# A delta-rule sandwich kernel: sums of a variance and its epsilon from GpSimd to ScalarE, and a list of their own for the steps of blocks between the chain's steps

## The chip, the cores and the metric

The kernel runs on one NeuronCore of a Trainium2 chip. The metric is the device time of one execution in microseconds (us). Of the kernel before, three runs are given: 2363.38, 2366.94 and 2370.86 us, median 2366.94. One further execution was taken with the hardware profiler; times inside the kernel come from it.

The engines are named as in the profile: PE is TensorE's matmuls and PEld its weight loads, DVE is VectorE, ACT is ScalarE, POOL is GpSimd, and SP is SyncE, on whose queue nearly all DMAs are issued. Each engine works through its instructions in the order in which they were issued to it.

## The reference

The input x is 4 sequences of 4096 tokens with 512 features, in float32. Two sublayers are computed, each as x + layernorm(f(layernorm(x))).

```python
# first sublayer, on h = layernorm(x): 16 heads of 32 features
rk = h_heads / max(norm(h_heads), 1e-12)      # keys to read with
wk = rk of the token before (zero for the first)
v = h @ Wv.T;  gate = sigmoid(h @ Wg.T);  beta = sigmoid(h @ Wb.T)
for each token t:                             # S: 32x32 state per sequence and head
    err = (v_t - wk_t @ S) * beta_t
    S   = S + outer(wk_t, err)
    o_t = (rk_t @ S) * gate_t
f(h) = o @ Wo.T
# second sublayer, on h = layernorm(x1)
xn = layernorm(h, eps 1e-3) * ln_gamma + ln_beta
w_q = weight rounded to -1, 0, 1;  y = clip(xn * 128 / gamma) @ w_q, scaled back
```

Every layernorm needs, for each token, a power -0.5 of a variance plus an epsilon: one number in each of 128 partitions.

## The kernel before, in words

**Units and the two halves of the work.** A unit is 32 tokens of each of the 4 sequences: 128 rows, one per partition. There are 128 units. Inside a unit the recurrence over 32 tokens is solved at once: a triangular 32x32 matrix per sequence and head (`nat`) is formed and inverted, and its inverse is applied to the unit. What belongs to a unit alone is the work of the *blocks*: load x, normalise (`x_stats`, `x_norm`, `keys`), transpose (`keys_turn`), norms of the keys (`key_squares`, `key_sums`, `key_norms`), values and gates (`values`, `values_out`, `values_rest`), the matrix (`grams`, `blocks`, `writes`, `masked`). What needs the state of the unit before is the *chain*: `predict` (ps_r, then r = v - ps_r), `apply` (ps_u), `errors` (ps_f, then e and o), `grow` (ps_ds, then the state), and behind it the output projection (`project`, `residual`), the second layernorm (`x1_stats`, `x1_norm`, `x1_turn`, `x1_scale`), the ternary matmul (`ternary_a`, `ternary_b`) and `finish`.

**The inverses.** The matrices of a group of units are inverted together on VectorE, by pairs of instructions (`pr` at L359, then `na` at L365) and a last copy of ones (L370). Groups have 4, 4, 6, 6 and then 8 units. The matrices pass through DRAM: `masked` stores them (`nat_d`), `gather` (L346) loads two units' worth into one of two buffers `na`, `keep` (L389) stores the inverted ones (`q_d`), and `fetch_inverse` (L396) loads them for the chain.

**What sets the order.** The order on every engine is written out by hand: `in_order` chains every instruction behind the one before on its engine. A *step* has a unit i of the chain, or none, and a unit k of the blocks. For each step a list of items is walked (L820 to L837): `plan` for a step of the chain, `late` once no blocks are left (k > 128), and `lead` for a step without a chain. An item names a function and which unit it is for; a bare number is a share of the inverse, and `inverses` issues as many of its instructions as make up that share of the group's due in this step. The first ten steps are without a chain. Then come units -2 and -1 of the chain, and from unit 0 to unit 7 every step of the chain is followed by one without it (a pair), until the blocks are 20 units ahead; from unit 8 on every step has both. For each group, `spans` holds the steps during which it is inverted, and `moves` says at the end of which step each gather and keep is issued.

**Sums of a variance and its epsilon.** They are made for each unit at four places: in `x_norm` (L171, `vpe_a`), in `project` through `rstd_of` (L100, `vpe_b`), in `x1_stats` (L556, `vpe_c`) and in `ternary_b` (L614, `vpe_y`). Each is a POOL instruction on 128x1 elements and is followed by POOL's power (L172, L95). `x_norm` also makes the negative mean, `negm`, on POOL (L173) and `nba` from it (L174). The variances of b, c and y come from ScalarE: `squares` (L522) squares 512 columns and reads an accumulator; those of a come from VectorE (L107). `rstd_b` is what VectorE's `residual` (L545, `xr`) waits for. Further down POOL's queue are the copy into `hN` (L202), which `values` needs, and `gates` (L305).

The buffers: PSUM has four rotating banks and one tile of four banks, which ps_gram and ps_ds share. The small tiles (`vpe`, `acc`, `mv`) rotate through six buffers each.

Of the kernel before, what the change touches and what calls it, by code (L numbers as in the profile page):

```python
# [8 lines left out]
F32 = mybir.dt.float32  # L9
AF = mybir.ActivationFunctionType  # L10
ALU = mybir.AluOpType
AX = mybir.AxisListType

P = 128
LN_EPS_OUTER = 1e-5
LN_EPS_FFN = 1e-3
# [6 lines left out]
def kernel(  # L23
# [22 lines left out]
    nc = tc.nc  # L46
    B, T, D = x.shape
# [3 lines left out]
    NU = T // DH  # L51
# [4 lines left out]
    const = ctx.enter_context(tc.tile_pool(name="const", bufs=1))  # L56
# [21 lines left out]
    negm = const.tile([P, NU], F32, name="negm")  # L78
# [4 lines left out]
    wq = const.tile([P, KC, D], F32, name="wq")  # L83
    beta = const.tile([P, 1], F32, name="beta")
    eps2 = const.tile([P, 1], F32, name="eps2")

    def bcast(ap, shape, axis):
        return ap.unsqueeze(axis).to_broadcast(shape)
# [4 lines left out]
    def power(pool, t, name):  # L93
        r = pool.tile([P, 1], F32, tag="rstd", name=f"rstd_{name}")
        nc.gpsimd.tensor_tensor(r, t, mhalf[:, 0:1], ALU.pow)  # L95
        return r

    def rstd_of(pool, var, eps, name):
        t = pool.tile([P, 1], F32, tag="vpe", name=f"vpe_{name}")
        nc.gpsimd.tensor_scalar_add(t, var, eps)  # L100
        return power(pool, t, name)

    def mean_var(pool, src, name):
# [6 lines left out]
    with ExitStack() as ph1:  # L110
# [24 lines left out]
        stat = ph1.enter_context(tc.tile_pool(name="stat", bufs=6))  # L135
        cx = [{} for _ in range(NU)]

        sizes = [4, 4, 6, 6]
        NP = 4
# [6 lines left out]
        half = D // 2  # L146
# [20 lines left out]
        def x_norm(i):  # L167
            mv = cx[i].pop("mv")
            c = slice(i, i + 1)
            t = stat.tile([P, 1], F32, tag="vpe", name=f"vpe_a{i}")  # L170
            nc.gpsimd.tensor_scalar_add(t, mv[:, 1:2], LN_EPS_OUTER)  # L171
            nc.gpsimd.tensor_tensor(rsa[:, c], t, mhalf[:, 0:1], ALU.pow)  # L172
            nc.gpsimd.tensor_scalar_mul(negm[:, c], mv[:, 0:1], -1.0)  # L173
            nc.gpsimd.tensor_tensor(nba[:, c], negm[:, c], rsa[:, c], ALU.mult)  # L174

        def normed(h, xt, i):
# [227 lines left out]
        def inverses(share):  # L404

            inv["due"] += share / inv["steps"]
            while inv["ops"] is not None and inv["done"] < inv["due"] - 1e-9:
                d = next(inv["ops"], None)
                if d is None:
                    inv["ops"] = None  # L410
                else:
                    inv["done"] += d
# [118 lines left out]
        def project(i):  # L531
            my = cx[i]
            oT = my.pop("oT")
            my["ps_wo"] = ps = bank(f"ps_wo_{i}")
            for k in range(KC):
                nc.tensor.matmul(  # L536
                    ps, lhsT=oT[:, k, :], rhs=woT[:, k, :], start=(k == 0), stop=(k == KC - 1)
                )
            var = squares(i, ps, "b", scale=D**-0.5)
            my["rs_b"] = rstd_of(stat, var, LN_EPS_OUTER, f"b{i}")  # L540

        def residual(i):
            my = cx[i]
# [6 lines left out]
        def x1_stats(i):  # L550

            my = cx[i]

            var = squares(i, my["x1"], "c", bias=negm[:, i : i + 1])
            t = stat.tile([P, 1], F32, tag="vpe", name=f"vpe_c{i}")
            nc.gpsimd.tensor_scalar(  # L556
                t, var, (1.0 + LN_EPS_FFN) / D, LN_EPS_OUTER * LN_EPS_FFN, ALU.mult, ALU.add
            )
            rs = power(stat, t, f"c{i}")
            nb = stat.tile([P, 1], F32, tag="nb", name=f"nb_c{i}")  # L560
            nc.gpsimd.tensor_tensor(nb, negm[:, i : i + 1], rs, ALU.mult)
            my["rs"], my["nb"] = rs, nb
# [44 lines left out]
        def ternary_b(i):  # L607
            my = cx[i]
            ternary_half(i, range(KC // 2, KC))
            my.pop("xn")  # L610
            ps = my["ps_y"]
            var = squares(i, ps, "y", scale=D**-0.5)
            t = stat.tile([P, 1], F32, tag="vpe", name=f"vpe_y{i}")
            nc.gpsimd.tensor_tensor(t, var, eps2, ALU.add)  # L614
            my["rs_y"] = power(stat, t, f"y{i}")

        def finish(i):
            my = cx[i]
# [76 lines left out]
        def ternary_centre():  # L695
# [13 lines left out]
        BACK, AHEAD = "chain's unit", "unit of the blocks"  # L709
        plan = (  # L710
            (AHEAD, 4, load), (BACK, 2, fetch), (BACK, 2, fetch_inverse), (BACK, 2, again),
            (BACK, 0, predict), (AHEAD, -1, blocks), (AHEAD, -1, writes), (BACK, -1, out_turn),
            (BACK, -3, x1_turn),
            (BACK, 0, apply), (BACK, -3, x1_scale), (AHEAD, -1, masked),
            (AHEAD, 1, key_sums), (AHEAD, 3, x_stats), (AHEAD, 1, key_norms),
            (AHEAD, 2, keys), (AHEAD, 2, key_squares), 0.38,
            (BACK, -4, ternary_a), (BACK, 0, errors), (BACK, -4, ternary_b), (BACK, 0, outputs),
            (AHEAD, 3, x_norm), 0.2, (BACK, 0, grow), (BACK, -2, x1_stats),
# [21 lines left out]
            (AHEAD, 2, keys_turn), (AHEAD, -1, gates_first), (AHEAD, -2, gates), (AHEAD, 0, grams), 0.3,  # L740
        )


        FAR = 4 * NP + 4
        START = sizes[0] + 6
        steps = [(None, k) for k in range(START)]

        k = START - 1
# [6 lines left out]
        at_k = {k: n for n, (_, k) in enumerate(steps)}  # L755
        at_i = {i: n for n, (i, _) in enumerate(steps) if i is not None}
        spans, moves = [], {}
        for g, (f, n) in enumerate(zip(firsts, sizes)):
            begin = max(at_k[f + n] + 2, spans[-1][1] if g else 0)
            end = at_i[f - 2]  # L760
            assert begin < end
            spans.append((begin, end))

            free = spans[g - 2][1] + sizes[g - 2] // 2 - 1 if g > 1 else 0
            for a in range(n // 2):
                free = max(at_k[f + 2 * a + 2], free)
                assert free < begin
                moves.setdefault(free, []).append((gather, g, a))
                moves.setdefault(end - 1 + a, []).append((keep, g, a))
                free += 1  # L770

        traced = nc.cur_bb.bb.instructions
# [47 lines left out]
        for n, (i, k) in enumerate(steps):  # L820
            for g, (begin, end) in enumerate(spans):
                if begin == n:
                    inv.update(ops=invert(g), done=0.0, due=0.0, steps=end - begin)
            for item in lead if i is None else plan if k <= NU else late:
                if isinstance(item, float):
                    inverses(item)
                    continue
                base = i if item[0] == BACK else k
                if base is not None:
                    do(item[2], base + item[1], *item[3:])  # L830
            if any(end == n + 1 for _, end in spans):
                inverses(1.0)
            for f, g, a in moves.get(n, ()):
                f(g, a)
            for f in between.get(n, ()):
                f()
            seen = in_order(seen)  # L837
# [31 lines left out]
        place, both, again_ = some(1), some(2), some(1)  # L869
# [121 lines left out]
```

## Time and profile before

| | before |
|---|---|
| median of three runs | 2366.94 us |
| the profiled execution | 2368.07 us |
| its span, first to last instruction | 2366.3 us |
| PE busy | 2239.2 us (95%), 22563 matmuls |
| DVE busy | 2034.9 us (86%) |
| ACT busy | 1734.6 us (73%) |
| POOL busy | 1726.8 us (73%) |
| granted TensorE clock, mean | 0.978 |

By stage (busy us of each engine):

| stretch, us | PE | DVE | ACT | POOL | granted clock |
|---|---|---|---|---|---|
| 0 to 60 | 43.50 | 36.93 | 42.53 | 42.50 | 0.94 |
| 60 to 120 | 34.74 | 52.80 | 28.51 | 50.40 | 0.83 |
| 120 to 180 | 49.66 | 46.72 | 36.36 | 46.39 | 0.80 |
| 180 to 240 | 48.13 | 50.22 | 34.99 | 47.16 | 0.80 |
| 240 to 300 | 54.69 | 50.43 | 41.83 | 50.23 | 0.94 |
| 300 to 360 | 53.96 | 51.18 | 41.27 | 50.06 | 0.94 |
| 600 to 1000 | 395.64 | 359.74 | 313.20 | 317.61 | 1.00 |
| 2300 to 2366 | 53.91 | 25.78 | 29.50 | 16.37 | 0.92 |

How to read the lines that follow in this document: a line of the order in time has its start and its length in us, the engine, the line of the program and the operation, output and inputs by the program's names, their shapes and the number of instructions; in square brackets is how long the engine stood idle before it and what released it. SPq is SP's queue, where DMAs are issued. The page's slices cut the span into 40 equal parts and give busy tenths, and the granted clock in tenths of full speed.

### The profile page before, as it was taken

To read this page: it belongs to the slowest core of one execution; us is meant where nothing else is said; L and a number is where in the kernel's file an instruction comes from. 1 tells how busy PE (TensorE), PEld (TensorE's weight loads), DVE (VectorE), ACT (ScalarE), POOL (GpSimd) and SP (SyncE) were. 2 spreads that over 40 slices of the span, in tenths; PEclk is the share of its full clock that TensorE was granted. 3 is DMA by queue.
4 is the path that set the end of the run, shared out by engine and by line. 5 is a ranking of instruction groups with operands and counts; after the bars stand their busy time and mean duration, and the time that the engine had idled before them with its cause. 6 is when DMAs were issued, how large, how long until landed. Compare 5 with 4: busy or idle time off the path is not lost.

```text
span 2366.3 us, 60183 instructions
## 1 busy us (share of the span) xinstructions
PE 2239.2 (95%) x22563; PEld 1459.4 (62%) x22563; DVE 2034.9 (86%) x3068; ACT 1734.6 (73%) x3485; POOL 1726.8 (73%) x2695
## 2 busy tenths in 40 slices
PE   7687889999999999999999999999999999989997
PEld 5465656656666666666666666666666666655553
DVE  6878888988898898989899898989989898899863
ACT  7466667777777777877777787877778787766774
POOL 7877887877878787877878787787878788643322
PEclk9878999999999999999999999999999999999999
DMA  6586577787878868787887878778787977776752
GB/s 186 136 187 171 161 187 188 192 187 188 187 212 192 221 178 209 203 188 213 191 219 179 212 197 197 207 192 215 180 214 197 198 203 191 193 170 160 188 154 85
DMA packets 753107, 445.27 MB, mean 188 GB/s; under 512 B 578832, under 2 KB 578832, under 8 KB 752816
## 3 DMA queue, kind: packets, MB, share of 16 engines
q1 hardware_dynamic: 752432, 440.90, 74.5%
q8 instruction: 178, 2.92, 0.5%
q14 instruction: 113, 0.93, 0.1%
q10 hardware_dynamic: 384, 0.52, 0.1%
HBM read 205.07 MB, written 235.14 MB: 186 GB/s over the span
## 4 chain that ended last, share of the span: by engine, by line
PE 73%; DVE 12%; POOL 5%; ACT 3%; issue 3%; DMA 2%; SPq 2%; ACTq 0%; DVEq 0%; POOLq 0%
PE ps_y L599 16%; PE ps_wo L536 15%; PE ps_v L246 8%; PE ps_v L274 7%; PE ps_ds L493 6%; PE ps_u L457 5%; PE ps_gram L314 4%; DVE pr L359 4%; PE ps_r L441 4%; PE ps_hT L191 3%; DVE na L365 3%; PE ps_oT L516 2%; PE ps_f L470 2%; PE ps_xn L516 1%; DVE r L447 1%
## 5 line engine op out<-in xcount | busy, mean ns | idle before, releaser
L599 PE MATMUL ps_y<-wq,xn 128*128 128x512 f32 x1024 | 502.9, 615 | 0.0
L359 DVE TENSOR_TENSOR pr<-na 128x336 f32<-128x336 f32 (+25 forms) x540 | 464.6, 860 | 18.3 <-DMA na<-nat_d 7.0
L325 ACT COPY nat<-ps_gram 32x512 f32<-32x512 f32 x512 | 295.2, 577 | 239.2 <-PE ps_gram L314 233.8
L536 PE MATMUL ps_wo<-woT,oT 128*128 128x512 f32 x1024 | 467.2, 599 | 0.4 <-ACT oT L529 0.4
L365 DVE TENSOR_TENSOR na<-na,pr 128x336 f32<-128x336 f32 (+25 forms) x540 | 454.3, 841 | 12.2
L226 POOL TENSOR_TENSOR rn<-ss,mhalf 128x16 f32<-128x16 f32 x128 | 425.7, 3326 | 10.7
L499 DVE TENSOR_TENSOR state<-ps_ds,state 32x512 f32<-32x512 f32 x508 | 348.4, 686 | 28.4 <-PE ps_ds L493 22.2
L430 ACT COPY tbd<-q 32x512 f32<-32x512 f32 x512 | 313.1, 611 | 7.0
L333 POOL TENSOR_TENSOR nat<-nat,mb 128x512 f32<-128x512 f32 x122 | 162.0, 1328 | 198.8 <-issue 190.0
L536 PEld LDWEIGHTS ps_wo<-woT,oT 128*128 128x128 f32 x1024 | 186.7, 192 | 190.0 <-issue 186.8
L246 PE MATMUL ps_v<-wvbT,hN 128*128 128x288 f32 x1024 | 280.8, 419 | 19.9 <-POOL hN L202 19.9
L599 PEld LDWEIGHTS ps_y<-wq,xn 128*128 128x128 f32 x1024 | 177.0, 193 | 152.6 <-issue 150.0
L246 PEld LDWEIGHTS ps_v<-wvbT,hN 128*128 128x128 f32 x1024 | 198.5, 196 | 116.9 <-issue 34.9
L274 PE MATMUL ps_v<-wvbT,hN 128*128 128x256 f32 x1024 | 242.9, 380 | 0.0
L274 PEld LDWEIGHTS ps_v<-wvbT,hN 128*128 128x128 f32 x1024 | 195.9, 191 | 34.2
L493 PEld LDWEIGHTS ps_ds<-e,h 32*128 32x128 f32 x4064 | 128.9, 191 | 111.2 <-DVE e L473 77.1
L581 ACT ACTIVATE xn<-ps_xn,lnb,lng 128x128 f32<-128x128 f32 x512 | 193.2, 465 | 0.2 <-PE ps_xn L516 0.2
L457 PE MATMUL ps_u<-tbd,r 128*32 128x128 f32 x4096 | 143.1, 282 | 47.9 <-DVE r L447 47.9
L545 DVE SCALAR_TENSOR_TENSOR xr<-ps_wo,rstd_b,xr 128x512 f32<-128x512 f32 x128 | 96.1, 750 | 98.9 <-POOL rstd_b L95 94.6
L493 PE MATMUL ps_ds<-e,h 32*128 32x128 f32 x4064 | 153.6, 289 | 15.0 <-DVE e L473 15.0
L522 ACT ACTIVATE junk_y<-ps_y 128x512 f32<-128x512 f32 x128 | 76.4, 597 | 120.0 <-PE ps_y L599 120.0
L457 PEld LDWEIGHTS ps_u<-tbd,r 128*32 128x32 f32 x4096 | 107.5, 112 | 71.1 <-DVE r L447 43.7
(152 smaller groups left out, 4027.2 us busy)
## 6 DMA issues: line engine op xcount, KB each, us to landing
x<-in_L_attn_x_dram SPq DMA_DIRECT2D x256, 128.0 KB
hT_d<-hT SPq DMA_DIRECT2D x128, 256.0 KB
v_d<-v SPq DMA_DIRECT2D x128, 256.0 KB
nat_d<-nat SPq DMA_DIRECT2D x128, 256.0 KB
na<-nat_d SPq DMA_DIRECT2D x256, 128.0 KB
q_d<-na SPq DMA_DIRECT2D x64, 512.0 KB
v<-v_d SPq DMA_DIRECT2D x128, 256.0 KB
hT<-hT_d SPq DMA_DIRECT2D x128, 256.0 KB
```

The costliest lines, as they stand in the source:

```text
L226: nc.gpsimd.tensor_tensor(rn, ss, mhalf, ALU.pow)
L246: nc.tensor.matmul(ps[:, : half + 2 * H], lhsT=my["hN"][:, k, :], rhs=wvbT[:, k, half:], start=(k == 0), stop=(k == KC - 1),)
L274: nc.tensor.matmul(ps[:, :half], lhsT=my["hN"][:, k, :], rhs=wvbT[:, k, :half], start=(k == 0), stop=(k == KC - 1),)
L325: nc.scalar.copy(nat[s].rearrange("p (j q) t -> p j q t", j=HQ), ps[s].rearrange("p j (q t) -> p j q t", q=NQ)[:, :, :, s],)
L359: nc.vector.tensor_tensor(prs[s], bcast(na[:, :, s, s + 1 :], [P, np_, s, m], 2), bcast(na[:, :, :s, s], [P, np_, s, m], 3), ALU.mult,)
L365: nc.vector.tensor_tensor(na[:, :, :s, s + 1 :], na[:, :, :s, s + 1 :], prs.pop(s), ALU.add)
L430: nc.scalar.copy(tbds[i % NBD][s, :, s], q[s])
L457: nc.tensor.matmul(ps[quarters(j), qq * P : (qq + 1) * P], lhsT=r[:, hd * DH : (hd + 1) * DH], rhs=tbd[:, j * NQ + qq, :], start=True, sto ...
L493: nc.tensor.matmul(psd[:, b, q * P : (q + 1) * P], lhsT=h[s, q * P : (q + 1) * P], rhs=e[s, q * P : (q + 1) * P], start=True, stop=True,)
L499: nc.vector.tensor_tensor(S[s, :, :, s], psd[s].rearrange("p b (q d) -> p b q d", q=NQ)[:, :, :, s], S[s, :, :, s], ALU.add,)
L536: nc.tensor.matmul(ps, lhsT=oT[:, k, :], rhs=woT[:, k, :], start=(k == 0), stop=(k == KC - 1))
L599: nc.tensor.matmul(my["ps_y"], lhsT=my["xn"][:, k * P : (k + 1) * P], rhs=wq[:, k, :], start=(k == 0), stop=(k == KC - 1),)
```

## The change

Three things are changed.

1. The four sums of a variance and its epsilon, and the negative mean, are ScalarE activations instead of POOL instructions. `rstd_of` now makes the sum with an Identity activation whose bias is a tile (`eps_a`, `eps_c` or `eps2`) and which can scale; `x1_stats` and `ternary_b` use it too. The powers, `nba` and `nb_c` stay on POOL.
2. A step without a chain that comes after the first ten walks a new list, `beside`. It differs from `lead` in its shares of the inverse: 0.3 ahead of `values_out` of the second half and 0.3 ahead of that of the first half, none at the end. In a step of the chain that is followed by such a step, the shares of `plan` are multiplied by 1.4.
3. For the first four groups, all keeps are issued at the end of the group's last step, and the gathers of the group that takes over the buffer may begin right behind that; for groups of eight it is as before.

```diff
+    eps_a = const.tile([P, 1], F32, name="eps_a")
+    nc.gpsimd.memset(eps_a, LN_EPS_OUTER)
+    eps_c = const.tile([P, 1], F32, name="eps_c")
+    nc.gpsimd.memset(eps_c, LN_EPS_OUTER * LN_EPS_FFN)
...
-    def rstd_of(pool, var, eps, name):
+    def rstd_of(pool, var, eps, name, scale=1.0):
+
         t = pool.tile([P, 1], F32, tag="vpe", name=f"vpe_{name}")
-        nc.gpsimd.tensor_scalar_add(t, var, eps)
+        nc.scalar.activation(t, var, AF.Identity, bias=eps, scale=scale)
         return power(pool, t, name)
...
-            nc.gpsimd.tensor_scalar_add(t, mv[:, 1:2], LN_EPS_OUTER)
+            nc.scalar.activation(t, mv[:, 1:2], AF.Identity, bias=eps_a)
+            nc.scalar.mul(negm[:, c], mv[:, 0:1], -1.0)
             nc.gpsimd.tensor_tensor(rsa[:, c], t, mhalf[:, 0:1], ALU.pow)
-            nc.gpsimd.tensor_scalar_mul(negm[:, c], mv[:, 0:1], -1.0)
...
-            my["rs_b"] = rstd_of(stat, var, LN_EPS_OUTER, f"b{i}")
+            my["rs_b"] = rstd_of(stat, var, eps_a, f"b{i}")
...
-            t = stat.tile([P, 1], F32, tag="vpe", name=f"vpe_c{i}")
-            nc.gpsimd.tensor_scalar(
-                t, var, (1.0 + LN_EPS_FFN) / D, LN_EPS_OUTER * LN_EPS_FFN, ALU.mult, ALU.add
-            )
-            rs = power(stat, t, f"c{i}")
+            rs = rstd_of(stat, var, eps_c, f"c{i}", scale=(1.0 + LN_EPS_FFN) / D)
...
-            t = stat.tile([P, 1], F32, tag="vpe", name=f"vpe_y{i}")
-            nc.gpsimd.tensor_tensor(t, var, eps2, ALU.add)
-            my["rs_y"] = power(stat, t, f"y{i}")
+            my["rs_y"] = rstd_of(stat, var, eps2, f"y{i}")
...
+        beside = (
+            (AHEAD, 4, load), (AHEAD, -1, blocks), (AHEAD, 3, x_stats), (AHEAD, 1, key_sums),
+            (AHEAD, 0, values), (AHEAD, 2, keys), (AHEAD, -1, writes), (AHEAD, 1, key_norms),
+            (AHEAD, 2, key_squares), (AHEAD, -1, masked), 0.3, (AHEAD, 0, values_out, half),
+            (AHEAD, 0, values_rest), (AHEAD, 3, x_norm), 0.3, (AHEAD, 0, values_out, 0),
+            (AHEAD, 2, keys_turn), (AHEAD, -1, gates_first), (AHEAD, -2, gates), (AHEAD, 0, grams),
+        )
...
+        def place(g, a):
+
+            return a if sizes[g] == 2 * NP else 0
+
...
-            free = spans[g - 2][1] + sizes[g - 2] // 2 - 1 if g > 1 else 0
+            free = spans[g - 2][1] + place(g - 2, sizes[g - 2] // 2 - 1) if g > 1 else 0
...
-                moves.setdefault(end - 1 + a, []).append((keep, g, a))
+                moves.setdefault(end - 1 + place(g, a), []).append((keep, g, a))
...
-            for item in lead if i is None else plan if k <= NU else late:
+            double = i is not None and n + 1 < len(steps) and steps[n + 1][0] is None
+            between_chain = i is None and n >= START
+            for item in (
+                plan if i is not None and k <= NU else late if i is not None
+                else beside if between_chain else lead
+            ):
                 if isinstance(item, float):
-                    inverses(item)
+                    inverses(1.4 * item if double else item)
                     continue
```

For comparison, the list `lead` that was walked in those steps before:

```python
lead = (
    (AHEAD, 4, load), (AHEAD, -1, blocks), (AHEAD, 3, x_stats), (AHEAD, 1, key_sums),
    (AHEAD, 0, values), (AHEAD, 2, keys), (AHEAD, -1, writes), (AHEAD, 1, key_norms),
    (AHEAD, 2, key_squares), (AHEAD, -1, masked), (AHEAD, 0, values_out, half), 0.35,
    (AHEAD, 0, values_rest), (AHEAD, 3, x_norm), (AHEAD, 0, values_out, 0), 0.35,
    (AHEAD, 2, keys_turn), (AHEAD, -1, gates_first), (AHEAD, -2, gates), (AHEAD, 0, grams), 0.3,
)
```

## The prediction, made before the changed kernel was run

> **What bounds the kernel now.** I read the page's slices first.
>
> ```profile
> PE   7687889999999999999999999999999999989997
> PEclk9878999999999999999999999999999999999999
> ```
>
> TensorE is full from slice 7 on; it idles, and runs at a lower granted clock, in the first 360 us. Then I read TensorE in order of time. Once the steps are regular, one follows the other every 17.01 us (ps_r at 361.38, 378.39, 395.40 us), and a step's matmuls fill it. So a step of the chain costs 17.01 us whatever the other engines do, unless TensorE waits. What the change can win is waits. They lie in four places.
>
> *Before the chain (25 to 75 us).* POOL works without a break here, 6.3 to 7.4 us a step, and TensorE waits for hN 0.15 to 1.9 us a step.
>
> *The pairs (127.45 to 361.38 us): eight times a chain's step and a step of blocks alone, then step 8.* TensorE, pair 6:
>
> ```profile
> 285.71 1.08 PE L441 MATMUL ps_r<-state,hT 128*32 128x128 f32 x32
> ...
> 290.45 1.43 PE L457 MATMUL ps_u<-tbd,r 128*32 128x128 f32 x32 [2.64 <-DVE r L447]
> ...
> 312.48 1.08 PE L441 MATMUL ps_r<-state,hT 128*32 128x128 f32 x32
> ```
>
> ps_u waits 2.64 us for r, then runs 1.43 us where 1.08 is usual: the clock had dropped. VectorE shows why r is late:
>
> ```profile
> 287.59 0.34 DVE L365 TENSOR_TENSOR na<-na,pr 128x174 f32<-128x174 f32 x1
> 287.97 1.25 DVE L359 TENSOR_TENSOR pr<-na 128x90 f32<-128x90 f32 x1
> 289.26 0.32 DVE L365 TENSOR_TENSOR na<-na,pr 128x90 f32<-128x90 f32 x1
> 289.49 0.28 DVE L370 COPY na<-diag 128x96 f32<-128x96 f32 x1
> 289.64 0.66 DVE L447 TENSOR_TENSOR r<-v,ps_r 128x512 f32<-128x512 f32 x1
> ```
>
> Operations of the inverse (lead's shares 0.35 and 0.3 behind the last values_out) stand in front of r. The nine waits for r sum to 26.7 us, those for ft and e in pairs 0 to 3 to 6.3, and matmuls at half clock run 23.1 us longer than the same ones at full clock (pair 1: u 1.93 for 1.08, f 1.11 for 0.60, ds 2.09 for 1.17, hT 1.11 for 0.66, wo 4.74 for 3.60, 3.9 us together). So 56 of these 233.9 us are waiting or half clock.
>
> *One DMA at 531 us.*
>
> ```profile
> 522.83 0.41 SPq L389 DMA_DIRECT2D q_d<-na  x1
> 523.29 5.12 SPq L346 DMA_DIRECT2D na<-nat_d  x4
> ```
>
> The last gather of group 5 is issued only behind the keep of group 4, when group 5 already begins. VectorE stands 6.95 us, TensorE 6.23, and its next matmul runs at half clock: that step lasts 547.13 - 521.13 = 26.0 us, 9.0 too long.
>
> *Once in each group of eight (601, 739, ... 1978 us, eleven times).* POOL:
>
> ```profile
> 731.36 1.10 POOL L556 TENSOR_SCALAR vpe_c<-acc_c 128x1 f32<-128x1 f32 x1
> 732.54 1.48 POOL L95 TENSOR_TENSOR rstd_c<-vpe_c,mhalf 128x1 f32<-128x1 f32 x1
> ...
> 734.69 0.23 POOL L100 TENSOR_SCALAR vpe_b<-acc_b 128x1 f32<-128x1 f32 x1
> 735.01 0.57 POOL L95 TENSOR_TENSOR rstd_b<-vpe_b,mhalf 128x1 f32<-128x1 f32 x1
> ```
>
> VectorE runs its two 128x960 operations from 731.26 to 733.61, and POOL's vpe_c, 0.19 us elsewhere, takes 1.10. So rstd_b is 2.25 us behind the accumulator (read until 732.76), VectorE idles 2.00 us before xr, r is late, ps_u waits 1.27 to 1.29 us. Eight steps take 137.67 us, not 136.08: 1.59 lost.
>
> **The change part by part.**
>
> *POOL to ScalarE.* Per unit POOL loses vpe_a, negm, vpe_y, vpe_c, vpe_b: 0.28 + 0.25 + 0.25 + 0.29 + 0.46 us mean and five gaps of 0.08, 1.9 us. ScalarE gains five 128x1 activations. No row shows one with a bias from a tile; the nearest are gb (128x32, 0.18 us, the next one starting 0.09 to 0.14 behind its start) and, for a bias tile, junk_c against sq (0.725 to 0.630: 0.10 more). So 0.28 us each and about 0.18 from start to start. The other end is xn (128x128, two operand tiles): 1.51 us for four, so 0.35 from start to start; the lower end is gb's 0.09. I take 0.18 (gb is nearest in size), and 0.12 more behind each accumulator read, because sq starts 0.84 to 0.86 behind h, which it reads, where tbd starts 0.72 behind. That is 1.2 us a step. ScalarE is busy 13.4 of 17.01 and waits 2.4 for ps_gram in most steps, so it has room.
>
> [...]
>
> What waits on this: four of the five stand ahead of junk_b, whose start goes back by 0.9 - 0.15 (ScalarE's idle before hT) = 0.73 us; then vpe_b and the pow, 0.39 us. So the pow starts 1.12 us behind the old end of the read. Over the nine steps from 613 to 751 us it started 1.08, 1.92, 1.34, 0.50, 0.43, 1.79, 2.08, 2.25 and 1.07 behind: two steps lose 0.65 us, and they have 1.0 of slack at r; the four late ones win 0.65 to 1.1. In the step that costs 1.59, rstd_c then runs ahead of the 128x960 pair, though nb_c or hN may still be held by it; r comes about 1 us earlier. I take 1.2 of 1.59: 11 x 1.2 = **13 us** (6 to 17.5). The tail's hops stay: 0.35 us from read to pow before, 0.3 to 0.39 after: 0.
>
> Before the chain, POOL's step is shorter by 0.62 us (two of 0.23, two gaps): five steps, **3 us** (0 to 4). From 75 us on VectorE is full, and nothing is won.
>
> In group 4 (412 to 521 us) six steps last 6.7 us longer than 17.01, bound by VectorE; of its idle 0.46 to 0.78 before xr I count 0.3 a step: **2 us** (0 to 4).
>
> *List beside, and 1.4.* A pair does 1.4 + 0.6 shares where it did 1 + 1: no instruction is added, 0.4 of a share moves to the chain's step, and the last inverse operation stands ahead of values_out 0, not behind it. r then waits only for ps_r. Cover for the moved share: a group of six costs about 36 us of VectorE over eight steps, 4.5 a share. In the chain's step 0.53 of it (2.4 us) lies ahead of e. r ends 1.85 us after ps_r's start, sums and statistics end at 3.15, so e at 5.6 to 6.4; ps_f allows e at 5.9. That may cost 0.5 us a pair. The next 0.50 (2.3 us) fits between gmax and xr, where VectorE waits now. In the step of blocks 0.3 (1.35 us) fits the 0.85 to 1.9 us in which VectorE now waits for gb.
>
> What is late next is VectorE itself. TensorE needs 17.01 + 5.40 (280.31 to 285.71) = 22.4 us for a full pair; VectorE is busy 22.3 to 23.9 us in pairs 4 to 7. So pairs 4 to 7 go from 28.40, 25.19, 26.77, 27.00 to about 23.3 each (14.2 won), step 8 from 21.90 to 17.8 (4.1). Pairs 1 to 3 have no ps_y to fill the waits for ft and e: VectorE's 20.8 to 22.8 busy plus 1.5 to 2.5 of waiting gives 23.5, 24, 24, from 27.42, 27.57, 27.26 (10.7); pair 0 from 22.42 to 20.5 (1.9). Sum 31; less 2 for e coming late, **29 us** (12 to 40; 40 if nearly all waits for r and half of the half clock go).
>
> Of these 29 us, 7.9 are half clock of pairs 4 to 8 (2.9, 1.65, 1.66, 1.66). I take them as gone with the waits, since in this trace matmuls ran slow right behind waits of 2.64, 2.87 and 3.17 us.
>
> *Gathers and keeps of the first four groups.* The same DMAs. keeps of a short group go out together, three of 512 KB, at its last step; the next gather into that buffer follows a step later, at least 17 us, and a keep takes 0.4 us to issue. Group 5's last gather goes out at the end of step 16 instead of 17, ahead of the keep: **9 us** (6 to 9). All else on SP's queue keeps its order.
>
> **Sum.** 3 + 29 + 2 + 9 + 13 = 56 us. The profiled execution took 2368.07 us (span 2366.3), 1.1 over the median of 2366.94: 2368.07 - 56 = 2312, and about 2311 beside the median.
>
> **Rivals.**
> 1. *ScalarE's delay eats the steady gain.* junk_b comes later, and the 128x960 operations still catch POOL. For: junk_b starts right behind tbd, so each insertion shows. Against: POOL is the late one in six of nine steps. 56 - 13 - 2: 2326 us.
> 2. *The pairs stay near 26 us,* because VectorE's stalls beside POOL's large operations (1.25 us for 0.3 above) now fall ahead of e, and the clock still drops. For: VectorE is 83% busy there. 5 us instead of 29: 2335 us.
> 3. *Slower.* Each 128x1 activation costs ScalarE far more than any row, because it waits out its predecessor. With c from start to start, xr moves by 5c - 0.05 - 1.38 (the mean delay above), and r has 0.73 us of slack: TensorE loses beyond c = 0.43 us, 5c - 2.16 in each of some 100 steps. Against 43 us won elsewhere the kernel is slower from c = 0.52; at 0.6 it loses 84, 2368 + 41 = 2409 us. Against: the dearest row is 0.35.
> 4. *The waits go, the half clock stays,* because something other than these waits sets it. For: behind the wait of 2.67 us in pair 5 there was none. Against: in pairs 6 to 8 it began right behind the wait. 56 - 7.9: 2320 us. [...]
> 5. *No net change:* rivals 1 and 2 and a gather that is late for another reason: 2360 to 2370 us.
>
> **Chances.** Forecast 0.53 (2292 to 2325), rival 1 0.15, rival 2 0.12, rival 3 0.08, rival 4 0.07, rival 5 0.05. The range 2291 to 2342 takes in the bounds of the terms (4 + 40 + 4 + 9 + 17.5 = 75 won at most, 0 + 12 + 0 + 6 + 6 = 24 at least) and rivals 1, 2 and 4. Within 0.3% (7 us, about what this measurement can tell): 0.05; faster 0.87; slower 0.08.
>
> **What would show it.** In the pairs: ps_u without [<-DVE r], pairs of 23 to 24 us, granted clock 1.0 from pair 4 on. No wait of na for nat_d. Eight steps in 136.1 to 136.5 us instead of 137.67. ScalarE 128x1 rows of 0.2 to 0.3 us, POOL busy 245 us less. I am wrong if ps_ds takes over the wait of ps_u (e late by over 1 us), or xr still waits 2 us for rstd_b.

## The result, and the profile after

The changed kernel takes 2324.16 us (median of five runs, 2323.82 to 2325.28) against 2366.94 (also of five: 2363.38 to 2370.86). The ratio is 0.982, with a 95% interval of 0.981 to 0.983. The profiled execution has a span of 2322.1 us against 2366.3: 44.2 us less, where the prediction's sum was 56. It lies inside the range of 2291 to 2342, 13 us above the forecast of 2311.

PE is busy 2222.8 us, DVE 2035.4, ACT 1856.7 (640 instructions and 122 us more) and POOL 1476.4 (250 us less; 245 were forecast). The page's slices:

```profile
PE   6678999999999999999999999999999999999997
PEclk9889999999999999999999999999999999999999
```

TensorE is now full from slice 5 on, where it was from slice 7. To see which term of the sum came true, the execution is cut at three places, each the start of a step (ps_r): unit 0's (pair 0), step 9's (the first regular step behind pairs and step 8), and the one behind the 26-us step. All values are us of the profiled execution:

| kernel | to pair 0 | pairs and step 8 | step 9 to the late gather's step | from there to the end |
|---|---|---|---|---|
| before | 127.5 | 233.9 | 185.8 | 1819.2 |
| after | 127.3 | 214.5 | 174.6 | 1805.8 |
| won | 0.2 | 19.4 | 11.1 | 13.5 |
| predicted | 3 | 29 | 11 (2 and 9) | 13 |

Two terms came out as forecast. The missing 12 us belong to the other two, nearly all of them to the pairs.

**The steady part.** POOL, in the step that answers to the one shown at 731 us of before; VectorE's two 128x960 operations now run from 699.46 to 701.80:

```profile
698.40 0.54 POOL L99 TENSOR_TENSOR rstd_c<-vpe_c,mhalf 128x1 f32<-128x1 f32 x1
699.02 0.19 POOL L562 TENSOR_TENSOR nb_c<-negm,rstd_c 128x1 f32<-128x1 f32 x1
...
701.89 0.54 POOL L99 TENSOR_TENSOR rstd_b<-vpe_b,mhalf 128x1 f32<-128x1 f32 x1 [2.35 <-ACT vpe_b L105]
```

rstd_c starts 1.06 us ahead of the wide operation and takes 0.54 (1.48 before); nb_c is through ahead of it as well. POOL then waits 2.35 us for vpe_b, so it is no longer late. VectorE waits 0.67 us ahead of xr (2.00 before), and ps_u 0.20 us for r where it waited 1.27. Eight steps take 136.62 us instead of 137.67, a little more than the 136.1 to 136.5 that were forecast.

**The late gather.** SP's queue, with the last gather of group 5 a step ahead of the first keep of group 4:

```profile
484.12 2.46 SPq L351 DMA_DIRECT2D na<-nat_d  x4
...
501.02 0.41 SPq L394 DMA_DIRECT2D q_d<-na  x1
```

The wait of na for nat_d is gone, and the 26.0-us step takes 17.02.

**The pairs.** Pair 6, TensorE and then VectorE:

```profile
277.79 0.66 PE L521 MATMUL ps_xn<-ident,h 128*128 128x128 f32 x4 [1.00 <-DVE v L267]
...
278.48 1.08 PE L462 MATMUL ps_u<-tbd,r 128*32 128x128 f32 x32
...
285.32 1.17 PE L498 MATMUL ps_ds<-e,h 32*128 32x128 f32 x32 [1.69 <-DVE e L478]
```

```profile
277.20 0.26 DVE L375 COPY na<-diag 128x96 f32<-128x96 f32 x1
277.33 0.40 DVE L267 TENSOR_TENSOR v<-ps_v,nrm 128x256 f32<-128x256 f32 x1
277.66 0.67 DVE L452 TENSOR_TENSOR r<-v,ps_r 128x512 f32<-128x512 f32 x1
```

The inverse's copy of ones stands ahead of the last v, and r right behind it. ps_u has no bracket, but ps_xn ahead of it waits 1.00 us for that v. The matmuls here have full clock (1.08, 1.17). The pairs took, in order, 25.82, 24.85, 26.35, 24.84, 23.59, 22.42, 25.50 and 22.75 us, and step 8 18.39. Pairs 4, 5 and 7 are near the forecast of 23.3 or below it. Pairs 0 to 3 and pair 6 are longer; pair 2 shows where the time is:

```profile
179.81 1.08 PE L462 MATMUL ps_u<-tbd,r 128*32 128x128 f32 x32 [0.22 <-DVE r L452]
181.60 0.66 PE L475 MATMUL ps_f<-ident,ft 128*128 128x128 f32 x4 [0.70 <-ACT ft L468]
186.43 2.09 PE L498 MATMUL ps_ds<-e,h 32*128 32x128 f32 x32 [4.17 <-DVE e L478]
```

Pair 2's wait of 3.84 us for r has become 0.22, but ps_ds waits 4.17 for e, and behind that wait it takes 2.09 where 1.17 is full clock. VectorE in the same pair:

```profile
181.17 0.54 DVE L364 TENSOR_TENSOR pr<-na 128x90 f32<-128x90 f32 x1
181.74 1.31 DVE L370 TENSOR_TENSOR na<-na,pr 128x90 f32<-128x90 f32 x1
...
185.28 0.49 DVE L370 TENSOR_TENSOR na<-na,pr 128x324 f32<-128x324 f32 x1
185.70 0.68 DVE L478 TENSOR_TENSOR e<-ps_f,bet 128x512 f32<-128x512 f32 x1
```

Eight operations of the inverse stand between the statistics and e, 4.5 us of them. The second, of a shape that took 0.32 us at 289.26 in before, took 1.31 beside POOL's nat (181.68 to 182.95 us). ps_f was done at 182.26, so e could have started 3.4 us earlier.

### The profile page after: what moved, and what is told of

Its sections match the earlier page's. It is cut to its first block, busy times and chain, and to the rows that moved or that the text cites. A ratio compares the mean times of both kernels' runs of the same rounds, so it can differ in the third digit from the quotient of the medians.

```text
span 2322.1 us, 59971 instructions
## 1 busy us (share of the span) xinstructions
PE 2222.8 (96%) x22563; PEld 1451.7 (63%) x22563; DVE 2035.4 (88%) x3068; ACT 1856.7 (80%) x4125; POOL 1476.4 (64%) x2057
## 4 chain that ended last, share of the span: by engine, by line
PE 74%; DVE 12%; ACT 5%; DMA 2%; POOL 2%; issue 2%; SPq 2%; ACTq 0%; DVEq 0%; POOLq 0%
PE ps_wo L541 16%; PE ps_y L600 15%; PE ps_v L251 9%; PE ps_v L279 8%; PE ps_ds L498 5%; PE ps_gram L319 5%; PE ps_r L446 5%; PE ps_u L462 4%; DVE pr L364 4%; PE ps_hT L196 3%; DVE na L370 2%; PE ps_oT L521 2%; PE ps_f L475 2%; PE ps_xn L521 2%; ACT tbd L435 1%
## 5 line engine op out<-in xcount | busy, mean ns | idle before, releaser
L600 PE MATMUL ps_y<-wq,xn 128*128 128x512 f32 x1024 | 494.7, 606 | 0.0
L231 POOL TENSOR_TENSOR rn<-ss,mhalf 128x16 f32<-128x16 f32 x128 | 440.6, 3442 | 10.7
L99 POOL TENSOR_TENSOR rstd_b<-vpe_b,mhalf 128x1 f32<-128x1 f32 x128 | 93.6, 731 | 331.3 <-ACT vpe_b L105 331.3
L600 PEld LDWEIGHTS ps_y<-wq,xn 128*128 128x128 f32 x1024 | 174.6, 190 | 149.3 <-issue 147.0
L452 DVE TENSOR_TENSOR r<-v,ps_r 128x512 f32<-128x512 f32 x128 | 87.7, 685 | 91.1 <-PE ps_r L446 90.7
## 6 DMA issues: line engine op xcount, KB each, us to landing
x<-in_L_attn_x_dram SPq DMA_DIRECT2D x256, 128.0 KB
na<-nat_d SPq DMA_DIRECT2D x256, 128.0 KB
```

Of the source, the lines that this page charges most:

```text
L231: nc.gpsimd.tensor_tensor(rn, ss, mhalf, ALU.pow)
L600: nc.tensor.matmul(my["ps_y"], lhsT=my["xn"][:, k * P : (k + 1) * P], rhs=wq[:, k, :], start=(k == 0), stop=(k == KC - 1),)
```

## The experiments

The first theory was that the three parts add up, each in its own stage. Three kernels make one part of the change each. The fourth is the changed kernel with part of the sums taken back.

**E1, the sums and the mean alone** (the diff down to `rs_y`, without the list and the places).

> The kernel before with the sums and the negative mean on ScalarE, nothing else. Main theory (the parts add up, each in its own stage): 13 us in the steady steps from 547 us on, 0 to 3 in group 4, 0 before the chain, so 2366.9 - 14 = 2353 us (2349 to 2356); eight steady steps take 136.1 to 136.4 us, ps_u waits under 0.3 us for r, the pairs keep their waits of 2.4 to 3.8 us and the 26-us step stays. Rival (the steady gain is one of phase: the earlier start of the steady part decides whether VectorE's 128x960 operations meet vpe_c): the waits of 1.27 us stay, under 4 us won, 2363 us or more.

Measured: 2353.2 us, 13.8 less than before; ratio 0.9945 (0.993 to 0.996). Stages: 128.0, 231.3, 183.3, 1805.8. ps_u waits 0.20 us where it waited 1.27, and the pairs keep their waits for r (2.2 to 4.7). The steady gain is the sums' work alone, wherever the steady part starts. The theory held here, and the rival of a mere shift in time did not.

**E2, the list and the factor 1.4 alone.**

> The kernel before with the list of the steps of blocks and the factor 1.4, nothing else. Main theory: the pairs and step 8 (233.9 us before, 214.5 in the changed kernel) win 19 to 23 us by this alone, a little more than in the whole change since pair 0 isn't held by a late xr; the 26-us step and the 1.27-us waits of each group of eight stay: 2344 to 2348 us. Rival (the list needs the lighter POOL, since its operations now fall where POOL's wide ones stretch VectorE's): under 12 us won, 2355 us or more.

Measured: 2361.7 us, only 5.3 less; ratio 0.998 (0.997 to 0.999). Stages: 129.5, 221.8, 189.1, 1819.6. The theory that the parts add up fell here. The pairs win 12.1 us in their stage and give back 3.3 in the next. The waits for r went (0.2 us or none, 1.3 in pair 0), but others took their place: for e in pairs 0 to 3 (1.8 to 3.9 us), and for hN in pairs 3 to 7 (1.4 to 3.4). TensorE in pair 4, and POOL at the same time:

```profile
245.10 3.16 PE L246 MATMUL ps_v<-wvbT,hN 128*128 128x288 f32 x8 [3.00 <-POOL hN L202]
```

```profile
241.08 1.20 POOL L172 TENSOR_TENSOR rsa<-vpe_a,mhalf 128x1 f32<-128x1 f32 x1
242.35 0.50 POOL L173 TENSOR_SCALAR negm<-mv_a 128x1 f32<-128x1 f32 x1
242.93 0.79 POOL L174 TENSOR_TENSOR nba<-negm,rsa 128x1 f32<-128x1 f32 x1
243.80 0.19 POOL L556 TENSOR_SCALAR vpe_c<-acc_c 128x1 f32<-128x1 f32 x1
244.07 0.56 POOL L95 TENSOR_TENSOR rstd_c<-vpe_c,mhalf 128x1 f32<-128x1 f32 x1
...
244.84 0.21 POOL L202 COPY hN<-hT 128x16 f32<-128x16 f32 x1
```

hN waits its turn behind the small operations of x_norm and x1_stats, and these are stretched besides (rsa 1.20 us and nba 0.79, where their medians in before are 0.56 and 0.19). With r no longer late, POOL is next in the pairs; of the sums' 1.9 us a unit, all but vpe_b's 0.5 stand ahead of hN. Step 9 also takes 20.8 us for 17.0, since xr comes late. The total and the point are the rival's: the list needs the lighter POOL.

**E3, the gathers and keeps alone.**

> The kernel before with the keeps and gathers of the first four groups moved, nothing else. Main theory: the 26-us step becomes 17.0 to 17.6 us, 9 won; pair 0 may lose up to 1 us (its loss of 3 in the changed kernel came mostly from VectorE being late, not from the second keep): 2357 to 2360 us. Rival A (the second keep ahead of the load of xr is what holds pair 0): 9 won and 3 lost, 2361 us. Rival B (the wait for the gather goes elsewhere): 2364 us or more.

Measured: 2361.4 us, 5.6 less; ratio 0.998 (0.997 to 0.9985). Stages: 127.4, 234.2, 176.7, 1819.9. The 26-us step takes 17.0 us, 9.0 won. Pair 0 takes 24.4 us where it took 22.4, with h<-xr starting at 128.36 behind a DMA wait (125.30 in before). The total is the one of rival A, but that rival isn't shown: in this trace the pairs' stage as a whole loses only 0.3 us.

**E4, the changed kernel with vpe_a and negm back on POOL.**

> The changed kernel with vpe_a and negm back on POOL; vpe_b, vpe_c and vpe_y stay on ScalarE. Theory 1 (the steady gain is vpe_c no longer run by POOL beside the 128x960 pair; vpe_a and negm, on ScalarE, only delay the prologue): eight steps stay at 136.1 to 136.5 us, the work before 26 us is about 3 us earlier again but the steps without a chain go back to 6.3 us, total 2322 to 2328 us. Theory 2 (every POOL instruction taken away counts, since POOL's queue as a whole was late): eight steps go to 136.7 or more, 5 to 12 us lost, 2329 to 2336 us.

Measured: 2328.9 us (2324.3 to 2332.6), 4.7 more than the changed kernel by the medians; ratio to before 0.983 (0.982 to 0.9845). Stages: 127.9, 222.7, 175.8, 1804.5. The steady part keeps all its gain, as theory 1 had it, and a little more: eight steps take 136.35 us, 136.62 in the changed kernel, and no ps_u waits there. In the trace the pairs lose 8 us: ps_v waits 1.7 to 2.8 us for hN again, in pairs 4, 5 and 7. So moving vpe_a and negm is worth nothing in the steady steps, and helps the list in the pairs. By how much stays open: the trace is of the longest execution (2332.6 us), two of the five (2324.3 and 2324.8) took no longer than the changed kernel, and the intervals of the two ratios overlap.

**E7, the list with vpe_a and negm on ScalarE, nothing else.** This asks the same of the other side.

> The kernel before with the list, the 1.4, and vpe_a and negm on ScalarE; vpe_b, vpe_c and vpe_y stay on POOL, and the gathers stay. New theory (with the list POOL is the next bound in the pairs, by hN behind the x_norm operations): the waits of ps_v for hN (1.4 to 3.4 us in pairs 3 to 7 of the list alone) nearly go, the pairs and step 8 take 8 to 10 us less than with the list alone; the 1.27-us waits of each group of eight stay, and the 26-us step: 2361.7 - 9 = 2353 us (2350 to 2356). Rival (all five sums count alike, so two of five give 0.4 of it): 2358 us or more.

Measured: 2340.7 us, 27.4 less, 12 more than the theory had; ratio 0.989 (0.987 to 0.9905). Stages: 127.5, 216.6, 186.4, 1806.8. The pairs win 5.2 us over the list alone, less than the 8 to 10 expected, and step 9 takes 18.4 instead of 20.8. The surprise is the last stage: with vpe_b, vpe_c and vpe_y still on POOL the steady part wins 12.4 of 13.5 us. ps_u waits 0.35, not 1.27. So in the steady steps it is enough to take either vpe_a and negm or the other three off POOL; what they win there doesn't add up.

**E9 and E11** ask why, each on the kernel before. E9 moves negm alone, which stands ahead of vpe_c on POOL; E11 moves vpe_b alone, which stands behind it. E9's edit:

```diff
+            nc.scalar.mul(negm[:, c], mv[:, 0:1], -1.0)
...
-            nc.gpsimd.tensor_scalar_mul(negm[:, c], mv[:, 0:1], -1.0)
```

> The kernel before with the negative mean alone on ScalarE (0.23 us and its gap, 0.31 us of POOL a step, ahead of vpe_c). Theory (the loss of 1.59 us in each group of eight is a matter of which comes first: vpe_c started at 593.69 us, 0.10 behind VectorE's 128x960 operation at 593.59, and was stretched to 1.10 us; started 0.3 earlier it is done in 0.19): the waits of 1.27 us for r become under 0.35 and the steady part wins 9 to 13 us by this alone, 2367 - 11 = 2356 us (2353 to 2359). Rival (what is won is POOL's time taken off, so one of five operations gives a fifth): 2 to 4 us, 2363 to 2365 us.

> The kernel before with vpe_b alone on ScalarE, which stands behind vpe_c on POOL, not ahead of it. Theory of which comes first: vpe_c still starts beside the 128x960 operation and is stretched to 1.1 us, its power to 1.4; only vpe_b's own 0.3 us is won at rstd_b, so the wait for r goes from 1.27 to about 0.95 us, 3 to 4 us won in all: 2363 to 2364 us. Rival (any operation taken off POOL ends the loss): 10 or more won, 2357 us or less.

Measured: E9 2359.9 us, 6.3 less (0.996 to 0.998), steady part 1812.5; E11 2362.75, 3.4 less (0.9975 to 0.999), steady part 1817.5. E11 came nearly as its theory had it (ps_u waits 1.02). E9 came between its two expectations (0.63). POOL in E9's costly step; VectorE's 128x960 pair runs from 594.18 to 596.53:

```profile
593.99 0.19 POOL L556 TENSOR_SCALAR vpe_c<-acc_c 128x1 f32<-128x1 f32 x1
594.26 1.47 POOL L95 TENSOR_TENSOR rstd_c<-vpe_c,mhalf 128x1 f32<-128x1 f32 x1
595.81 0.77 POOL L561 TENSOR_TENSOR nb_c<-negm,rstd_c 128x1 f32<-128x1 f32 x1
```

And in E11's, where VectorE's pair starts at 591.82:

```profile
591.93 1.09 POOL L558 TENSOR_SCALAR vpe_c<-acc_c 128x1 f32<-128x1 f32 x1
593.10 1.48 POOL L97 TENSOR_TENSOR rstd_c<-vpe_c,mhalf 128x1 f32<-128x1 f32 x1
```

vpe_c slipped in ahead of the wide operation in E9, by 0.19 us, and took 0.19 instead of 1.09. But the power behind it did not, and nb_c was caught instead of the first. It is a matter of which starts first, as the theory said, but instruction by instruction: in these traces each of the pair's two operations catches one instruction of POOL, the first that starts while it runs. E7's costly step goes one further. There vpe_c starts 0.66 us ahead of the pair; vpe_c and rstd_c take their own time, and nb_c (0.96, where 0.19 is its shortest in before) and gr (1.14 for 0.21, further down) are caught:

```profile
576.30 0.19 POOL L560 TENSOR_SCALAR vpe_c<-acc_c 128x1 f32<-128x1 f32 x1
576.58 0.54 POOL L99 TENSOR_TENSOR rstd_c<-vpe_c,mhalf 128x1 f32<-128x1 f32 x1
577.19 0.96 POOL L565 TENSOR_TENSOR nb_c<-negm,rstd_c 128x1 f32<-128x1 f32 x1
```

In the changed kernel nothing between rstd_c and rstd_b is caught. With vpe_c 0.10 us behind the pair's start (before), 0.19 ahead (E9), 0.66 ahead (E7) and gone, ps_u waits 1.27, 0.63, 0.35 and 0.20 us.

**E5: e first.** Now the pairs' shortfall. The shares of a chain's step in a pair are 0.15, 0.5, 0.66 and 0.09 instead of 0.53, 0.28, 0.50 and 0.08.

```diff
-                    inverses(1.4 * item if double else item)
+                    inverses(apart[item] if double else item)
```

> The changed kernel with the shares of a chain's step in a pair moved behind e: 0.15, 0.5, 0.66, 0.09 instead of 0.53, 0.28, 0.50, 0.08 (same sum). Theory (the pairs that are left over 23 us wait for e behind the inverse's operations, 4.5 us of them at 181 us): ps_ds waits 3.5 to 4.2 us less 2 to 3 in pairs 1 to 3 and under 0.5 in pairs 4 and 6, full clock comes back there, pairs 1 to 3 go from 24.9, 26.4, 24.8 to about 23.3, total 5 to 8 us less: 2316 to 2319 us. Rival (VectorE's whole work in a pair is the bound): the wait goes over to r, xn or xr, total within 2 us of the changed kernel's 2324.

Measured: 2321.1 us (2318.6 to 2322.6), 3.1 less than the changed kernel by the medians; ratio to before 0.980 (0.979 to 0.982). Pairs and step 8 take 211.0 us. The waits of ps_ds of 3.5 to 4.2 us are 0.8 to 1.7, so the cause of the late e is right, and pairs 1 to 3 take 72.1 us instead of 76.0. But pair 1 alone takes 26.6, as ps_u waits 2.13 for r there, and pairs 4 to 7 take 96.3 us together, 2.0 more than in the changed kernel: ps_xn waits 0.4 to 1.1 us for v there, ps_v 0.5 for hN or 0.7 for xr. Both theories have a part. In pairs 2 and 3 the order was the limit. In pairs 4 to 7, where ps_y fills TensorE ahead of ps_ds, a share put later delays something else.

**E6: the first xr two steps earlier on SP's queue.**

```diff
+            if n == START - 2:
+                do(again, 0)
```

> The changed kernel with the first load of xr issued two steps earlier on SP's queue, ahead of keep, x and q. Theory (pair 0 starts 3 us late because h waits for xr and tbd and gb stand behind h on ScalarE): h no longer waits 3.2 us for the DMA, pair 0 goes from 25.8 to 22 to 23 us, total 2320 to 2322 us. Rival (tbd's q lands as late as xr, so tbd holds gb all the same): pair 0 over 25 us, total 2323 to 2325.

Measured: 2319.8 us, 4.4 less than the changed kernel by the medians; ratio to before 0.980 (0.979 to 0.9815), which only just meets the changed kernel's interval. Pairs and step 8 take 211.1 us, 3.4 less, nearly all of it won in pair 0: 22.53 us for 25.82, the others alike to 0.1. ScalarE in the changed kernel, then in this one:

```profile
128.43 0.81 ACT L183 ACTIVATE h<-xr,nba,rsa 128x512 f32<-128x512 f32 x1 [3.16 <-DMA xr<-in_L_attn_x_dram]
129.15 2.52 ACT L435 COPY tbd<-q 32x512 f32<-32x512 f32 x4
131.69 0.20 ACT L256 ACTIVATE gb<-ps_v 128x32 f32<-128x32 f32 x1
```

```profile
125.29 0.82 ACT L183 ACTIVATE h<-xr,nba,rsa 128x512 f32<-128x512 f32 x1
126.01 2.52 ACT L435 COPY tbd<-q 32x512 f32<-32x512 f32 x4
128.56 0.20 ACT L256 ACTIVATE gb<-ps_v 128x32 f32<-128x32 f32 x1
```

The wait for xr is gone, and everything behind it on ScalarE comes 3.1 us earlier, gb among it, for which VectorE's v and so r had waited. tbd's q had landed already.

**E8: the keeps of groups 0 and 1, and the gathers that take over their buffers, as before the change.**

```diff
-            return a if sizes[g] == 2 * NP else 0
+            return a if g < 2 or sizes[g] == 2 * NP else 0
```

> The changed kernel with the keeps and gathers moved for groups 2 and 3 only, those of groups 0 and 1 as before the change. Theory (the second keep of group 0, issued ahead of x, q and xr, is what makes pair 0 late): pair 0 takes 21 to 23 us instead of 25.8, the step at 516 us stays at 17.0, total 2320 to 2322 us. Rival (pair 0 is late since VectorE ends the first inverse 2 us later, whatever the keeps): pair 0 over 25 us, 2323 to 2326 us.

Measured: 2322.7 us (2321.5 to 2324.1); ratio 0.981 (0.980 to 0.9825), not told apart from the changed kernel's. Pair 0 takes 23.9 us, with ps_u still waiting 4.48 for r, and pair 1 23.2. Inconclusive: neither expectation is met. ps_u's wait in pair 0 lies between 2.4 and 5.7 us in every kernel of this study with xr where it was, except E2's 1.3 (E11, with the old gathers, has 4.0); in the three with xr early it is 0.9 to 2.6. So xr's load is the lever. How much the moved keep adds to its lateness stays open.

**E10: both mends,** E6's load and E5's shares for pairs 0 to 3 alone.

```diff
-                    inverses(1.4 * item if double else item)
+                    inverses(item if not double else apart[item] if i < 4 else 1.4 * item)
```

> The changed kernel with xr's first load two steps earlier, and the shares 0.15, 0.5, 0.66, 0.09 in the chain's steps of pairs 0 to 3 only. Theory (the two mends are in different pairs and add up: 3.3 of pair 0, 5.5 of pairs 1 to 3): 2313 to 2317 us, all pairs between 21 and 25.5. Rival (the work moved behind e is late for xr or v instead, and what pair 0 wins pair 1 loses): 2318 to 2320, as with one mend.

Measured: 2316.05 us (2314.1 to 2318.0); ratio to before 0.979 (0.978 to 0.980), below the changed kernel's 0.981 to 0.983. This version is faster than the changed kernel. Stages: 127.4, 204.8, 174.6, 1805.6. Pairs 0 to 3 take 89.4 us instead of 101.9, less evenly than expected: pair 0 takes 17.7, and pair 1 takes 26.8, with ps_u waiting 2.13 us for r, so the rival has a part. Pairs 4 to 7, whose lists did not change, take 97.0 instead of 94.3: part of the gain is paid back. Why is not shown; work that VectorE still has in hand is the likely reason.

**E12: less in the steps of blocks.** As E10, with the second 0.3 of `beside` halved and the chain's step at 1.55.

> The kernel with both mends, and the share ahead of the last values_out of a step of blocks halved from 0.3 to 0.15; the chain's step takes 1.55 for it: 0.15, 0.55, 0.75, 0.10 in pairs 0 to 3 and 0.40, 0.50, 0.56, 0.09 in pairs 4 to 7. Theory (in pairs 4 to 7 and step 8 ps_xn waits 0.4 to 1.07 us because the last values_out, which frees its bank, stands behind that share, and ps_ds 0.7 to 1.7 because e stands behind the other): both waits go in most pairs, 2 to 4 us less than 2316: 2312 to 2314 us. Rival (VectorE, 88 to 90% busy here, has no room left, so the wait goes to xr or r): 2315 to 2319 us.

Measured: 2317.2 us; ratio 0.979 (0.978 to 0.981), the same as E10. Pairs and step 8 take 208.2 us, step 9 17.8. The waits for v and e shrink to 0.2 to 0.5 and up to 1.1 us, and ps_v waits 1.1 to 1.6 us for hN in four pairs. Two rows of this stage, of E12 and of E10:

```profile
127.00:335.00 208.00, 188.64 (x1946) 132.07 (x1946) 191.64 (x305) 157.35 (x342) 176.09 (x224) 0.95 0.79 196
127.40:332.20 204.80, 185.23 (x1948) 129.68 (x1944) 183.83 (x303) 157.57 (x340) 172.74 (x224) 0.97 0.81 200
```

After the length come the busy times of PE, PEld, DVE, ACT and POOL, with the number of instructions in brackets. In E12 VectorE is busy 191.6 us of 208, more than TensorE. The rival is right in its total; the waits did move, though to hN more than to xr or r, which it named. But in E10 nearly the same operations of VectorE take 183.8 us. So VectorE's busy time changed by 7.8 us with the order here, for two instructions more; the likely reason, not shown, is what runs beside POOL and is stretched. No bound is shown by E12's row, and whether another order would win more stays open.

## Why the prediction was right, and where it was wrong

*Direction and size.* The direction, the range and the mechanism of three terms were right. None of the rivals came true in full, but rival 2's mechanism, VectorE stretched beside POOL ahead of e, is seen in pairs 1 to 3 (na on 128x420 takes 1.54 us in pair 1, on 128x90 1.31 in pair 2, and pr on 128x660 1.79 in pair 3; the next operation, of about the same size, takes 0.57, 0.34 and 0.84). The sum was 12 us too large, 9.6 of it in the pairs and 2.8 before them.

*POOL to ScalarE, 13 us: right (13.5), by the mechanism named.* A sum takes 0.28 to 0.29 us on ScalarE, and the next instruction starts 0.19 to 0.20 behind its start (0.18 was taken); for negm it is 0.19 and 0.09. In most steps junk_b starts 13.65 us behind its step's ps_r instead of 13.12: 0.53 later, where 0.73 was worked out. The price of rival 3, 0.43 us from start to start, is far away. The closeness of the total is part luck: the costly step of each group of eight wins 1.07 us where 1.2 was taken, about 11.4 in all with three steps that lose 0.12, and the other 2 us come from the last 18 steps and the tail, where the prediction had nothing. What the prediction missed is that the gain saturates: E7 has nearly all of it with two of five operations, and E9 shows that the loss goes in steps, one POOL instruction at a time.

*Gathers and keeps, 9 us, and group 4, 2 us: right* (9.0; 108.7 us for six steps became 106.6). That all else on SP's queue keeps its order was wrong: keeps and gathers of earlier groups changed place too. What that cost could not be told apart from what delays xr anyway (E8).

*The pairs, 29 us: wrong by 9.6.* Against the forecast of each, pair 0 is 5.3 us too long, pairs 1 to 3 together 4.5, pairs 4 to 7 1.1 and step 8 0.6; 2 had been allowed for e. Four statements of that step are to be held against the runs.
- "r then waits only for ps_r" and "ps_u without [<-DVE r]": right from pair 1 on, though in pair 6 and step 8 ps_xn ahead of ps_u waits 1.0 us for v. The granted clock is 1.00 from 215.7 us on, through pairs 4 to 7. They sum to 94.3 us against 93.2, step 8 took 18.4 against 17.8.
- "That may cost 0.5 us a pair" (e coming late): this is one of the two steps that failed. The waits for e are 3.5 to 4.2 us in pairs 1 to 3, which took 76.0 us where 23.5, 24 and 24 were forecast. Both ends of the estimate were off. There e starts 7.2 to 7.8 us behind ps_r instead of 5.6 to 6.4, and ps_f ends 4.3 to 4.5 behind it, where 5.9 was taken. The share ahead of e was too small, because 36 us were taken for a group of six. In before's trace a group of four takes that (35.2 and 35.6 us); the group of six from 184 to 289.5 us takes 49.7, 6.2 a share, so 0.53 of it is 3.3 us and not 2.4:

```profile
L359 DVE TENSOR_TENSOR pr<-na 128x90 f32<-128x90 f32 (+14 forms) x30 | 24.9, 831 | 0.7
L365 DVE TENSOR_TENSOR na<-na,pr 128x90 f32<-128x90 f32 (+14 forms) x30 | 24.5, 816 | 0.7
```

The 4.5 us of pair 2 are about 3.3 us of operations, rounded up to a whole one, and 1.2 of stretching beside POOL. And with ps_ds's waits of 3.5 to 4.2 us the clock goes to half again (from 161.06, 184.96 and 212.26 us; ps_ds takes 2.09 us for 1.17), which was counted as won. The prediction's own sign of being wrong, ps_ds taking over the wait of ps_u, is what is seen; E5 and E10 show that order is the cause.
- Pair 0 "from 22.42 to 20.5": it took 25.8, and this is the other step that failed. It was held in the first place by ScalarE's gb behind h, which waits for xr's DMA, and not by r's place behind the inverse. The DMA wait stood in before's trace (2.58 us) and was not followed. E6 takes it away: 3.3 us. With E5's shares besides (E10) pair 0 takes 17.7, so the order had a part there too.
- "What is late next is VectorE itself": incomplete. E2 shows that POOL is next, by hN. The list alone wins 12.1 us in the pairs' stage, not 29, and 5.3 in all. The 19.4 of the whole change need the other part, which lightens POOL at the same spot (E7: 5.2 us more in this stage, 27.4 in all); the sum treated the two as independent, and that it came this near is luck in that respect. E1 and E2 win 19.1 us together, with E3 24.7, and the whole change 42.8.

*Before the chain, 3 us: wrong (0.2).* The prediction priced POOL's shorter steps and took what stands at 75 us over to 127. The steps did get shorter: ps_gram follows ps_gram in 5.4 to 5.5 us between 64 and 75 us. But the first ps_gram started at 26.26 us instead of 22.73 (25.63 in E1), so the two meet at 75.13 and 75.31 us, and from there VectorE is the bound, busy 49.2 of the 52.0 us to pair 0. The delay goes with vpe_a on ScalarE: the eight kernels that have it there start the first ps_gram at 24.7 to 27.6 us, the six others at 22.7 to 24.3, by one trace of each. How vpe_a delays it was not followed. It matters little, since pair 0 starts between 127.1 and 129.5 us in all fourteen kernels.

*Rival 4, the clock.* In the stretch from 127 to 340 us the granted clock went from 0.87 to 0.94. It went back to full where the waits went (1.00 from 215.7 us on) and still went to half where ps_ds waits 3.5 us and more, so here the clock followed the waits. The prediction's reading, that waits of 2.6 to 3.2 us are enough, is borne out by most rows of the fourteen traces; the last paragraph has them.

## What to carry to other kernels

Two savings that sit on two engines of the same step are not two terms of a sum: ask of each what is late next, engine by engine, with the other saving and without it. When work is moved ahead of an operation, count the whole instructions that will stand there, at the size that they have in that stage, and add what they lose to a neighbour engine, instead of taking an average share. And where a small operation of one engine is caught by a wide one of another, starting a few tenths of a microsecond earlier can be worth more than the work that was taken off (E9: 0.31 us off POOL, 0.64 us off ps_u's wait).

## What the runs showed of the hardware

*128x1 operations on POOL beside VectorE's 128x960 ones.* In before, vpe_c at 593.69 us started 0.10 behind VectorE's 128x960 operation and ended at 594.79, 0.05 behind its end at 594.74; the power behind it started 0.10 behind the next one and ended 0.41 behind its end, close to its own time without company (0.54). Started 0.19 ahead of it, vpe_c took 0.19 (E9). So where VectorE started first, the POOL instruction was held until VectorE's had ended; E9's power (started 0.08 behind, ended 0.40 behind the end) and E7's nb_c (0.23 and 0.04) are alike. The rows don't show what holds it. Where POOL's power starts first, no hold of VectorE is seen: in E7 the power runs from 576.58 to 577.12 us, and VectorE's first operation starts at 576.96 and takes its usual 1.15, as far as the rough spans of POOL can tell.

*The clock and the length of a wait.* Over the fourteen kernels, between 127 and 560 us, the first group of matmuls behind a wait of 3.43 us or more (ps_u, ps_ds or ps_v, 32 cases) always ran slower, by 1.4 to 2.0 times. Behind the 54 waits of 1.9 to 3.3 us, 26 first groups ran slower, by 1.3 times or more. The granted clock itself tells more than the first group. Of the 54 waits, it went to half in 46, during the wait or up to 2.2 us behind its end; in two it was at half already, and in six it stayed up. In before it went to half in seven of eight, and stayed up behind the 2.67 us of pair 5. In E3 a wait of 3.24 us was followed by a group at full clock, and the half clock came 1.96 us behind the wait. Of the 67 waits of 1.0 to 1.9 us, it went to half behind six. So here waits of 1.9 to 3.3 us were mostly enough, and shorter ones mostly not. In the traces of before and after, every stretch between two changes of the granted clock is a multiple of 3.41 us (half from 291.03 to 294.45 us in before, for one), so where a wait falls among these steps may decide between the cases; no run isolates that.
